# Two of sixteen states multiplied by B on GpSimd, and side work moved between product and scan

## The chip, the core and the metric

The kernel runs on one core of one Trainium2 chip. A core has five engines with queues of their own, each working in order: TensorE (PE, with its weight loads shown as PEld), VectorE (DVE), ScalarE (ACT), GpSimd (POOL) and SyncE (SP), which here issues the DMAs. They meet through semaphores. SBUF and PSUM are on-chip memories of 128 partitions; PSUM has 16 KB in each partition and all of it is in use here. The metric is the device time of one execution in microseconds (us); lower is better.

## What is computed

Four layers work on four images of 64 x 64 pixels with 96 channels. Each layer has a mixer and a quantised feed-forward block, both with a norm before and a residual after. Layer 0 has a gated mixer of its own. Layers 1 to 3, which take most of the time, have a selective scan in four directions over the 4096 pixels with 192 inner channels and 16 states. Cut to what matters:

```python
xz = x @ in_proj_w.T
xi, z = jnp.split(xz, 2, axis=-1)
...
xc = jax.nn.silu(xc)                                   # after a 3x3 depthwise convolution
x0 = xc.reshape(Bsz, Di, L)                            # pixels row by row
x1 = jnp.transpose(xc, (0, 1, 3, 2)).reshape(Bsz, Di, L)   # column by column
xs = jnp.stack([x0, x1, x0[..., ::-1], x1[..., ::-1]], axis=1)
x_dbl = jnp.einsum('bkdl,kcd->bkcl', xs, x_proj_weight)
dts, Bs, Cs = jnp.split(x_dbl, [R, R + N], axis=2)
...
dt = jax.nn.softplus(delta + delta_bias[None, :, None])
dA = jnp.exp(dt4[..., None] * A4[None, :, :, None, :])
dBu = dt4[..., None] * u4[..., None] * Bt[:, :, None, :, :]
h = a * h + b                                          # the scan along the pixels
y = jnp.einsum('lbkdn,lbkn->lbkd', hs, C_l)
return y + u * Dskip[None, :, None]
```

After the scan the four directions are added, normalised, multiplied by silu(z) and projected back to 96 channels.

## The kernel before, in words

**Stages and jobs.** Layer 0 runs first (`gated`). Then there are 12 stages, layers 1 to 3 times four images, and each is one run of scans (`scans`, line 863). Everything else that an image needs between two scans (joining the orders, mixer output, feed-forward, norm, input projection, convolution) is written as generators that stop at each `yield`; they are gathered in a `Job` (line 711) that works one image ahead. `Job.step` adds a rate, 1.4, to a credit at every scan tile and gives each of its chains one step per whole credit. At line 1006 a stage that is close to its end runs its job to completion before it loads the next image's u.

**Items and tiles.** A stage has 24 items: two directions along the pixels (`d`) x four segments of T = 1024 pixels x three chunks of channels. A chunk fills the 128 partitions with two halves of 64 channels, each with an order, 0 for rows of pixels and 1 for columns: `CHUNKS` (line 37). Chunk 1 has its halves the other way round than the other two, order 1 below. An item has 16 tiles, one for each state n, so there are 12 x 24 x 16 = 4608 scan tiles of 128 x 1024.

**A tile.** The decay `da` is an exponential on ScalarE (`decays`, line 894), two tiles ahead, into one of three SBUF buffers. B comes as a row per state; TensorE spreads it over the partitions with a selection matrix `sel` into PSUM (`b_rows`, line 900, one tile ahead; `wide()` has two PSUM buffers). `scan` (line 910) multiplies it in place by `du` and runs the scan `h`, both on VectorE. The first or last column of `h` is kept for the next segment (`carry`, ScalarE). C comes as a row too: the rows are written to DRAM (`sg.cs`), and SP reads each back spread over 64 partitions, two transfers of 256 KB a tile, two tiles ahead (`c_rows`, line 884; four buffers). GpSimd multiplies h by c in place (`times_c`, line 935), and TensorE adds it into a PSUM accumulator (`accumulate`, line 955). h has four buffers.

**The order in a step.** The loop at line 994 emits, for tile k: carry(k-1); c rows and decay of k+2; B of k+1; product and scan of k; C product of k-1; now and then a store; then the side work: one step of the preparation of the next chunk, of the next segment, and of the job (`pump(chain)`, `pump(segment)`, `work()`); last the accumulation of k-2. Every engine keeps this order, which a wrapper (`InOrder`, whose line 80 is therefore the line of all instructions in the profile) writes out by hand. Side work of VectorE thus stands after the scan of its tile.

**Preparation and side work that the change touches.** `prepare_chunk` (line 814) has four large products on GpSimd for each item, issued at steps 5, 8, 11 and 13 of the item before. `prepare_segment` (line 766) projects u to B rows, delta rows and 48 rows for C: 16 for each half of the partitions in the order 0, 1, 0, so that either order of halves finds its rows. `Norm.measure` (line 235) calls `moments` (line 217): four statistics and four aggregations in one go. `convolve` (line 568) applies Silu to two tiles, writes u to DRAM and copies it, column by column, into `cols_a` and `part_c` with three copies on GpSimd. `logarithms` (line 253) does the pending logarithms of the norms on ScalarE.

Of the kernel before, what the change touches and what calls it, by code (L numbers as in the profile page):

```python
# [20 lines left out]
C = 96  # L21
# [12 lines left out]

CHUNKS = (((0, 0), (64, 1)), ((0, 1), (64, 0)), ((128, 0), (128, 1)))


NB3 = 96  # L40
NC3 = 48
XPW = NB3 + 2 * R + NC3
W_IN = 0
# [58 lines left out]
def metaformer(ctx: ExitStack, tc: tile.TileContext, x, l0_ab, l0_rest, ssm, ffn, out):  # L102
# [61 lines left out]
    make_identity(nc, ident)  # L164
    stacked = const("stacked", [128, 64])
    dve.tensor_copy(stacked[0:64], ident[0:64, 0:64])
    dve.tensor_copy(stacked[64:128], ident[64:128, 64:128])
    twice = const("twice", [128, 128])
    dve.tensor_copy(twice[:, 0:64], stacked)
    dve.tensor_copy(twice[:, 64:128], stacked)  # L170

# [3 lines left out]
    dve.tensor_tensor(mod32, mod32, ident[0:NB3, 64:96], ALU.add)  # L175
    sel = const("sel", [NB3, NS, 192], BF16)
    for n in range(NS):
        for k in range(3):
            at = NS * (k % 2) + n
# [36 lines left out]

    def moments(src, width):

        st = sb(5, "st", [128, G, 6])
        mv = sb(5, "mv", [128, G, 2])  # L220
        for g in range(G):
            dve.bn_stats(st[:, g, :], src[:, g, 0:width])
        for g in range(G):
            dve.bn_aggr(mv[:, g, :], st[:, g, :])
        return mv

    class Norm:
# [7 lines left out]
        def measure(self, src, width, e):  # L235

            mv = moments(src, width)
            yield
            act.activation(self.v, mv[:, :, 1], AF.Identity, bias=small[e])
            act.activation(self.nm, mv[:, :, 0], AF.Copy, scale=-1.0)  # L240
            pending.append(self)

        def settle(self):

            act.activation(self.r, self.r, AF.Exp, scale=-0.5)
            yield
            refine(self.r, self.v)
            pool.tensor_tensor(self.nm, self.nm, self.r, ALU.mult)


# [161 lines left out]
    def load_y(im, s, hold):  # L412
        t = slice(s * MM, (s + 1) * MM)
        yr, yc = sb(3, "pad0", [128, MM]), sb(3, "pad1", [64, MM])
        sp.dma_start(out=yc, in_=im.y[2, 0:64, t])
        sp.dma_start(out=yr[0:64], in_=im.y[0, 0:64, t])
        sp.dma_start(out=yr[64:128], in_=im.y[1, 64:128, t])
        hold["in"][s] = yr, yc
# [17 lines left out]
    def feed_forward(im, layer, s, hold, dst):  # L436
# [49 lines left out]
        yield  # L486
        x2 = sb(1, "x2", [128, G, C])
        pool.tensor_tensor(x2, x1, y, ALU.add)
# [79 lines left out]
    def convolve(im, layer, s, hold):  # L568
# [10 lines left out]
        for i, group in enumerate(groups):  # L579
            ps = bank("conv")  # L580
            for at, (lhs, rhs) in enumerate(group):
                pe.matmul(ps, lhs, rhs, start=at == 0, stop=at == len(group) - 1)
                yield
            v = sb(1, f"u{i}", [128, MM])
            act.copy(v, ps)
            release()
            yield i == 0
            raw.append(v)
        for i, v in enumerate(raw):
            act.activation(v, v, AF.Silu, bias=w[:, W_CB + i : W_CB + i + 1])  # L590
# [5 lines left out]
        sp.dma_start(out=im.u[0, 0:64, t], in_=raw[0][0:64])  # L596
        sp.dma_start(out=im.u[1, 64:128, t], in_=raw[0][64:128])
        sp.dma_start(out=im.u[2, 0:64, t], in_=raw[1][0:64])
        for p, src, dst, c0, nc_ in (
            (slice(0, 128), raw[0], cols_a, 0, HW),  # L600
            (slice(0, 64), raw[1], part_c, 0, HW // 2),
            (slice(64, 128), raw[1], part_c, HW // 2, HW // 2),
        ):
            pool.tensor_copy(
                dst[p].rearrange("p (c r) -> p r c", r=HW)[:, SR * s : SR * s + SR, :],
                src[p].rearrange("p (r c) -> p r c", c=HW)[:, :, c0 : c0 + nc_],
            )
            if p.start or p.stop == 128:
                yield
        if s == NSTRIP - 1:  # L610
            yield
            sp.dma_start(out=im.u[1, 0:64, :], in_=cols_a[0:64])
            sp.dma_start(out=im.u[0, 64:128, :], in_=cols_a[64:128])
            for k in range(2):
                sp.dma_start(
                    out=im.u[2, 64:128, k * L // 2 : (k + 1) * L // 2],
                    in_=part_c[64 * k : 64 * k + 64],
                )

    def between(im, layer, dst=None):  # L620
# [8 lines left out]
        def first():  # L629
            if layer:  # L630
                cols_a, part_c = hold["cols"] = columns()
                sp.dma_start(out=cols_a[0:64], in_=im.y[1, 0:64, :])
# [121 lines left out]
    def load_segment(item):  # L754
# [7 lines left out]
        sg.bs = sb(2, "bs", [NB3, T], BF16)  # L762
        sg.cs = dram.tile([NC3, T], F32, tag="cs", name="cs")
        return sg

    def prepare_segment(item, sg):
# [38 lines left out]
        for k in range(2):  # L805
            cols = slice(k * MM, (k + 1) * MM)
            yield True
            ps = bank("x_proj_c")
            yield from project(ps, m, m + NC3, k)
            act.copy(sg.rows[0:NC3, cols], ps[0:NC3])  # L810
            release()
        sp.dma_start(out=sg.cs, in_=sg.rows[0:NC3])

# [49 lines left out]
    def scans(stages, jobs):  # L863
# [14 lines left out]
        drain(Chain(prepare_chunk(items[0]), True))  # L878
        tiles = [(i, n) for i in items for n in range(NS)]
        live = {}  # L880
        carries = {}
        per = 2 * NSEG * 3

        def c_rows(k):
            i, n = tiles[k]
            c = live[k, "c"] = sb(4, "c", [128, T])
            for half in range(2):
                row = NS * (CHUNKS[i.chunk][0][1] + half) + n
                sp.dma_start(
                    out=c[64 * half : 64 * half + 64],  # L890
                    in_=i.sg.cs[row : row + 1, :].to_broadcast([64, T]),
                )

        def decays(k):
            i, n = tiles[k]
            da = live[k, "da"] = sb(3, "da", [128, T])
            at = (3 * i.d + i.chunk) * NS + n
            act.activation(da, i.delta, AF.Exp, scale=weights[i.layer].decay[:, at : at + 1])

        def b_rows(k):  # L900
            i, n = tiles[k]
            b = live[k, "b"] = wide()
            swap = CHUNKS[i.chunk][0][1]
            for half in range(2):
                cols = slice(half * MM, (half + 1) * MM)
                pe.matmul(
                    b[:, cols], sel[:, n, 64 * swap : 64 * swap + 128], i.sg.bs[:, cols], start=True, stop=True
                )

        def scan(k):  # L910
            i, n = tiles[k]
# [4 lines left out]
            i.carry = carries[i.chunk]  # L916
            dve.tensor_tensor(b, i.du, b, ALU.mult)
            h = live[k, "h"] = sb(4, "h", [128, T])
# [58 lines left out]

        last = len(tiles) - 1
        chain = segment = None
        c_rows(0)  # L980
        c_rows(1)
# [12 lines left out]
        for k in range(last + 4):  # L994
            q, n = divmod(k, NS)
            if k <= last:
# [9 lines left out]
                if item.chunk == 1 and n == 4 and at(q + 2) is not None:  # L1006
# [5 lines left out]
                    segment = Chain(next_segment(items[q + 2 : q + 5]))  # L1012
                if n == 11:
                    logarithms()
                if n == 8 and nxt is not None and nxt.d == 1:
                    nxt.yf = sb(2, "y", [128, T])
                    sp.dma_start(out=nxt.yf, in_=nxt.im.y[nxt.chunk, :, nxt.seg * T : (nxt.seg + 1) * T])
            if 0 <= k - 1 <= last:
                carry(k - 1)
            if k + 2 <= last:  # L1020
                c_rows(k + 2)
                decays(k + 2)
            if k + 1 <= last:
                b_rows(k + 1)
            if k <= last:
                scan(k)
# [12 lines left out]
            if 0 <= k - 2 <= last:  # L1039
                accumulate(k - 2)  # L1040
# [278 lines left out]
def _scan(in_w, conv_w, conv_b, xp_w, dt_w, dt_b, A_logs, Ds, ln_w, ln_b, out_w):  # L1319
# [5 lines left out]
    for d in range(2):  # L1325
        for chunk, halves in enumerate(CHUNKS):
            for k, (ch, order) in enumerate(halves):
# [4 lines left out]
                v[:, NB3 + R * order : NB3 + R * order + R] = t[:, :R]  # L1332
                for s in range(3):
                    if s % 2 == order:
                        v[:, m + NS * s : m + NS * s + NS] = t[:, R + NS :]
    w[:, W_XP:W_SSM] = xp.reshape(128, -1)
# [68 lines left out]
```

## Time and profile before

| | |
|---|---|
| three runs | 20,565.64, 20,566.9 and 20,584.47 us; median 20,566.9 |
| profiled execution | 20,577.35 us; span 20,575.5 us |
| mean granted TensorE clock | 0.824 |
| first scan tile to last | 2317 to 20,104 us of the span |
| one stage of 384 tiles | 1432 to 1563 us |
| busy share of the span | DVE 87%, PE 81%, POOL 75%, ACT 60%, PEld 24% |
| C rows | 9216 transfers of 256 KB, 4.1 us from issue to landing (median) |
| bytes moved by DMA | 3149 MB |

A share of busy time is a mean over layer 0, the scans and the end. In the scan part most of VectorE's time is two large groups, product and scan; the profile gives for every group the busy time, the mean duration of one instruction in ns, and the idle time of the engine just before it with what ended most of it. In the names, buffer numbers are left out: `bc` is the PSUM tile with B, `da` the decay, `h` the scan's result, `c` the spread C row, `cs` the C rows in DRAM.

### The profile page before, as it was taken

To read this page: it belongs to the slowest core of one execution; us is meant where nothing else is said; L and a number is where in the kernel's file an instruction comes from. 1 tells how busy PE (TensorE), PEld (TensorE's weight loads), DVE (VectorE), ACT (ScalarE), POOL (GpSimd) and SP (SyncE) were. 2 spreads that over 40 slices of the span, in tenths; PEclk is the share of its full clock that TensorE was granted. 3 is DMA by queue.
4 is the path that set the end of the run, shared out by engine and by line. 5 is a ranking of instruction groups with operands and counts; after the bars stand their busy time and mean duration, and the time that the engine had idled before them with its cause. 6 is when DMAs were issued, how large, how long until landed. Compare 5 with 4: busy or idle time off the path is not lost. (4 is left out here: it accounts for less than half of the span.)

```text
span 20575.5 us, 221152 instructions
## 1 busy us (share of the span) xinstructions
PE 16595.2 (81%) x70656; PEld 4890.0 (24%) x70656; DVE 17820.2 (87%) x13851; ACT 12306.0 (60%) x19377; POOL 15531.4 (75%) x10471
## 2 busy tenths in 40 slices
PE   7888788788788887888888888887788788887876
PEld 3333212121121222222222222222222222222223
DVE  5554699999999999999999999998999999999881
ACT  3443466665665665666665665665665666666553
POOL 2332588888888887888888888887888888888882
PEclk9999888787797888787788787787897887888775
DMA  0000366667667667666667666666666666676661
GB/s 18 13 16 15 97 171 185 164 174 183 163 179 184 163 173 184 160 177 185 163 174 186 162 181 182 164 178 172 162 183 179 167 189 166 171 189 163 167 172 46
DMA packets 1234531, 3148.69 MB, mean 153 GB/s; under 512 B 428048, under 2 KB 428176, under 8 KB 1227216
## 3 DMA queue, kind: packets, MB, share of 16 engines
q1 hardware_dynamic: 1233360, 3134.55, 57.7%
q8 instruction: 555, 9.09, 0.2%
q14 instruction: 616, 5.05, 0.1%
HBM read 2819.18 MB, written 314.57 MB: 152 GB/s over the span
## 5 line engine op out<-in xcount | busy, mean ns | idle before, releaser
L80 POOL TENSOR_TENSOR h<-h,c 128x1024 f32<-128x1024 f32 (+1 forms) x4992 | 11321.2, 2274 | 4296.3 <-ACT carry L80 1700.9
L80 DVE TENSOR_TENSOR_SCAN h<-da,carry,bc 128x1024 f32<-128x1024 f32 x4608 | 10814.7, 2347 | 608.6 <-POOL carry L80 10.4
L80 PE MATMUL acc<-h,stacked 64*64 64x512 f32 x36864 | 6206.0, 750 | 499.0 <-POOL h L80 494.0
L80 ACT ACTIVATE da<-delta,decay 128x1024 f32<-128x1024 f32 x4608 | 5280.8, 1147 | 1651.2 <-DVE h L80 1603.5
L80 DVE TENSOR_TENSOR bc<-du,bc 128x1024 f32<-128x1024 f32 x4608 | 5574.9, 1210 | 607.0 <-PE bc L80 580.7
L80 PE MATMUL bc<-bs,sel 96*128 96x512 bf16 x9216 | 3359.8, 453 | 2072.3 <-DVE h L80 2055.4
L80 ACT COPY carry<-h 128x1 f32<-128x1 f32 x3456 | 648.6, 188 | 3545.9 <-DVE h L80 3541.6
L80 PEld LDWEIGHTS <-sel 96*128 96x128 bf16 x9216 | 551.5, 101 | 7014.0 <-DVE h L80 5083.4
L80 PEld LDWEIGHTS acc<-h,stacked 64*64 64x64 f32 x36864 | 1134.2, 153 | 3292.2 <-issue 1687.8
L80 ACT ACT_TABLE_LOAD x1137 | 1458.8, 1283 | 42.6 <-DVE mv L80 23.5
L80 PE MATMUL conv<-pad,tap_lo 128*128 128x512 f32 x1728 | 915.6, 628 | 0.0
L80 PE MATMUL dt_proj<-rows,w 12*128 12x512 f32 x1152 | 816.7, 795 | 0.0
L80 ACT ACTIVATE c<-acc,l_bias 128x512 f32<-128x512 f32 x384 | 263.6, 687 | 906.1 <-PE acc L80 905.6
L80 ACT ACTIVATE du<-e,ones 128x1024 f32<-128x1024 f32 x576 | 660.7, 1147 | 231.1 <-POOL delta L80 225.5
L80 PE MATMUL x_proj_b<-u,xp 128*108 128x512 f32 x1152 | 670.9, 698 | 98.1 <-DMA xp<-in_ssm 58.4
L80 PE MATMUL acc<-h,fold 128*96 128x512 f32 x768 | 416.9, 625 | 366.0 <-ACT c L80 294.4
L80 POOL TENSOR_TENSOR delta<-delta,du 128x1024 f32<-128x1024 f32 x288 | 679.3, 2359 | 12.0 <-ACT du L80 12.0
L80 POOL TENSOR_TENSOR e<-e,du 128x1024 f32<-128x1024 f32 x288 | 679.7, 2360 | 2.4 <-ACT du L80 2.4
L80 POOL TENSOR_TENSOR du<-delta,u 128x1024 f32<-128x1024 f32 x288 | 679.6, 2360 | 0.7
L80 POOL TENSOR_TENSOR delta<-delta,e 128x1024 f32<-128x1024 f32 x288 | 678.8, 2357 | 0.1
L80 PE MATMUL x_proj_c<-u,xp 128*48 128x512 f32 x1152 | 620.5, 651 | 63.4 <-ACT rows L80 63.3
L80 PE MATMUL conv<-pad,tap_hi 128*128 128x512 f32 (+1 forms) x1152 | 636.7, 647 | 8.2 <-ACT u L80 8.2
(154 smaller groups left out, 15920.2 us busy)
## 6 DMA issues: line engine op xcount, KB each, us to landing
c<-cs SPq DMA_DIRECT2D x9216, 256.0 KB, 4.1
u<-u SPq DMA_DIRECT2D x288, 512.0 KB, 7.6
y<-y SPq DMA_DIRECT2D x1152, 128.0 KB, 2.4
y<-y SPq DMA_DIRECT2D x144, 512.0 KB, 5.9
xr<-x SPq DMA_DIRECT2D x224, 192.0 KB, 4.7
u<-u SPq DMA_DIRECT2D x288, 128.0 KB, 4.6
pad<-y SPq DMA_DIRECT2D x288, 128.0 KB, 4.6
z<-zl SPq DMA_DIRECT2D x96, 256.0 KB, 2.0
```

What stands on the lines that cost most here:

```text
L80: ins = f(*a, **k).ins
```

## The change

Seven edits go together:

- States 3 and 11 (`ON_POOL`) get their B row as C gets its own: two more rows for each half in `sg.cs`, read back by SP into an SBUF tile `b` (`pool_rows`, four tiles ahead, one buffer), and GpSimd multiplies it by `du` (`times_b`, two tiles ahead). Neither TensorE's spreading nor VectorE's product is issued for these tiles.
- The decay of these tiles takes the PSUM buffer that B would have had, and is issued one tile ahead.
- Chunk 1 turns its halves round, so every chunk has order 0 below. The 48 rows become 36, `sel` shrinks from 192 to 128 columns, and u and y of chunk 1 lie the other way round in DRAM.
- The side work of a step is emitted inside `scan`, between the product and the scan. The C product of k-1, the store, and the pending logarithms move ahead of or behind neighbours in the step's order.
- `Norm.measure` yields after every second statistic.
- The convolution waits with its Silu while a step with a GpSimd product two tiles ahead is on, and the three column copies go from GpSimd to ScalarE.
- The rate of the jobs goes from 1.4 to 1.6.

```diff
-CHUNKS = (((0, 0), (64, 1)), ((0, 1), (64, 0)), ((128, 0), (128, 1)))
+CHUNKS = (((0, 0), (64, 1)), ((64, 0), (0, 1)), ((128, 0), (128, 1)))
+ON_POOL = (3, 11)
...
-NC3 = 48
-XPW = NB3 + 2 * R + NC3
+NCO = NS + len(ON_POOL)
+NC2 = 2 * NCO
+XPW = NB3 + 2 * R + NC2
...
         def measure(self, src, width, e):
 
-            mv = moments(src, width)
+            st = sb(5, "st", [128, G, 6])
+            mv = sb(5, "mv", [128, G, 2])
+            for g in range(G):
+                dve.bn_stats(st[:, g, :], src[:, g, 0:width])
+                if g % 2:
+                    yield
+            for g in range(G):
+                dve.bn_aggr(mv[:, g, :], st[:, g, :])
             yield
...
+        yield lambda: all((step["n"] + 2 - n) % NS for n in ON_POOL)
         for i, v in enumerate(raw):
             act.activation(v, v, AF.Silu, bias=w[:, W_CB + i : W_CB + i + 1])
...
-            pool.tensor_copy(
+            act.copy(
                 dst[p].rearrange("p (c r) -> p r c", r=HW)[:, SR * s : SR * s + SR, :],
...
+        def from_rows(i, dst, at):
+
             for half in range(2):
-                row = NS * (CHUNKS[i.chunk][0][1] + half) + n
+                row = NCO * half + at
                 sp.dma_start(
-                    out=c[64 * half : 64 * half + 64],
+                    out=dst[64 * half : 64 * half + 64],
                     in_=i.sg.cs[row : row + 1, :].to_broadcast([64, T]),
                 )
 
+        def on_pool(k):
+            return k <= last and tiles[k][1] in ON_POOL
+
+        def pool_rows(k):
+            i, n = tiles[k]
+            b = live[k, "b"] = sb(1, "b", [128, T])
+            from_rows(i, b, NS + ON_POOL.index(n))
+
+        def times_b(k):
+            i, b = tiles[k][0], live[k, "b"]
+            pool.tensor_tensor(b, i.du, b, ALU.mult)
+
         def decays(k):
             i, n = tiles[k]
-            da = live[k, "da"] = sb(3, "da", [128, T])
+            da = live[k, "da"] = wide() if on_pool(k) else sb(3, "da", [128, T])
...
-        def scan(k):
+        def scan(k, beside):
...
-            dve.tensor_tensor(b, i.du, b, ALU.mult)
+            if not on_pool(k):
+                dve.tensor_tensor(b, i.du, b, ALU.mult)
+            beside()
             h = live[k, "h"] = sb(4, "h", [128, T])
...
-            if 0 <= k - 1 <= last:
-                carry(k - 1)
-            if k + 2 <= last:
-                c_rows(k + 2)
-                decays(k + 2)
-            if k + 1 <= last:
-                b_rows(k + 1)
-            if k <= last:
-                scan(k)
-            if 0 <= k - 1 <= last:
-                times_c(k - 1)
-            if k >= 3 and (k - 3) % NS == NS - 1:
-                store(items[(k - 3) // NS])
-            if k <= last:
+            step["n"] = n
+
+            def beside():
                 pump(chain)
                 pump(segment)
...
+            if 0 <= k - 1 <= last:
+                carry(k - 1)
+            if on_pool(k + 1):
+                decays(k + 1)
+            if k + 2 <= last:
+                c_rows(k + 2)
+                if not on_pool(k + 2):
+                    decays(k + 2)
+            if on_pool(k + 4):
+                pool_rows(k + 4)
+            if n == 11:
+                logarithms()
+            if k + 1 <= last and not on_pool(k + 1):
+                b_rows(k + 1)
+            if 0 <= k - 1 <= last:
+                times_c(k - 1)
+            if on_pool(k + 2):
+                times_b(k + 2)
+            if k >= 3 and (k - 3) % NS == NS - 1:
+                store(items[(k - 3) // NS])
+            if k <= last:
+                scan(k, beside)
             if 0 <= k - 2 <= last:
                 accumulate(k - 2)
...
-            jobs[-1].append(Job(between(im, layer - 1), 1.4))
+            jobs[-1].append(Job(between(im, layer - 1), 1.6))
```

More of the change, by code (lines that the diff above doesn't have):

```diff
@@ L164, in metaformer @@
     make_identity(nc, ident)
-    stacked = const("stacked", [128, 64])
-    dve.tensor_copy(stacked[0:64], ident[0:64, 0:64])
-    dve.tensor_copy(stacked[64:128], ident[64:128, 64:128])
     twice = const("twice", [128, 128])
-    dve.tensor_copy(twice[:, 0:64], stacked)
-    dve.tensor_copy(twice[:, 64:128], stacked)
+    for k in range(2):
+        p = slice(64 * k, 64 * k + 64)
+        dve.tensor_copy(twice[p, 0:64], ident[p, p])
+        dve.tensor_copy(twice[p, 64:128], ident[p, p])
+    stacked = twice[:, 0:64]
     mod32 = sb(4, "h", [NB3, 32])
@@ L175, in metaformer @@
     dve.tensor_tensor(mod32, mod32, ident[0:NB3, 64:96], ALU.add)
-    sel = const("sel", [NB3, NS, 192], BF16)
+    sel = const("sel", [NB3, NS, 128], BF16)
     for n in range(NS):
-        for k in range(3):
-            at = NS * (k % 2) + n
+        for k in range(2):
+            at = NS * k + n
             dve.tensor_copy(
@@ L214, in metaformer @@
         ffw.append((w1, w2, b))
[L217 to L225, printed above, removed]
     class Norm:
@@ L248, in settle @@
             pool.tensor_tensor(self.nm, self.nm, self.r, ALU.mult)
+    step = {"n": 0}
     pending = []
@@ L416, in load_y @@
         sp.dma_start(out=yr[0:64], in_=im.y[0, 0:64, t])
-        sp.dma_start(out=yr[64:128], in_=im.y[1, 64:128, t])
+        sp.dma_start(out=yr[64:128], in_=im.y[1, 0:64, t])
         hold["in"][s] = yr, yc
@@ L486, in feed_forward @@
         yield
-        x2 = sb(1, "x2", [128, G, C])
+        x2 = sb(1, "xh", [128, G, C])
         pool.tensor_tensor(x2, x1, y, ALU.add)
@@ L596, in convolve @@
         sp.dma_start(out=im.u[0, 0:64, t], in_=raw[0][0:64])
-        sp.dma_start(out=im.u[1, 64:128, t], in_=raw[0][64:128])
+        sp.dma_start(out=im.u[1, 0:64, t], in_=raw[0][64:128])
         sp.dma_start(out=im.u[2, 0:64, t], in_=raw[1][0:64])
@@ L611, in convolve @@
             yield
-            sp.dma_start(out=im.u[1, 0:64, :], in_=cols_a[0:64])
+            sp.dma_start(out=im.u[1, 64:128, :], in_=cols_a[0:64])
             sp.dma_start(out=im.u[0, 64:128, :], in_=cols_a[64:128])
@@ L631, in first @@
                 cols_a, part_c = hold["cols"] = columns()
-                sp.dma_start(out=cols_a[0:64], in_=im.y[1, 0:64, :])
+                sp.dma_start(out=cols_a[0:64], in_=im.y[1, 64:128, :])
                 sp.dma_start(out=cols_a[64:128], in_=im.y[0, 64:128, :])
@@ L762, in load_segment @@
         sg.bs = sb(2, "bs", [NB3, T], BF16)
-        sg.cs = dram.tile([NC3, T], F32, tag="cs", name="cs")
+        sg.cs = dram.tile([NC2, T], F32, tag="cs", name="cs")
         return sg
@@ L808, in prepare_segment @@
             ps = bank("x_proj_c")
-            yield from project(ps, m, m + NC3, k)
-            act.copy(sg.rows[0:NC3, cols], ps[0:NC3])
+            yield from project(ps, m, m + NC2, k)
+            act.copy(sg.rows[0:NC2, cols], ps[0:NC2])
             release()
-        sp.dma_start(out=sg.cs, in_=sg.rows[0:NC3])
+        sp.dma_start(out=sg.cs, in_=sg.rows[0:NC2])
     def prepare_chunk(item):
@@ L879, in scans @@
         tiles = [(i, n) for i in items for n in range(NS)]
+        last = len(tiles) - 1
         live = {}
@@ L886, in c_rows @@
             c = live[k, "c"] = sb(4, "c", [128, T])
+            from_rows(i, c, n)
+        def from_rows(i, dst, at):
             for half in range(2):
-                row = NS * (CHUNKS[i.chunk][0][1] + half) + n
+                row = NCO * half + at
                 sp.dma_start(
-                    out=c[64 * half : 64 * half + 64],
+                    out=dst[64 * half : 64 * half + 64],
                     in_=i.sg.cs[row : row + 1, :].to_broadcast([64, T]),
                 )
+        def on_pool(k):
[7 more added lines that the diff above has]
+            pool.tensor_tensor(b, i.du, b, ALU.mult)
         def decays(k):
             i, n = tiles[k]
-            da = live[k, "da"] = sb(3, "da", [128, T])
+            da = live[k, "da"] = wide() if on_pool(k) else sb(3, "da", [128, T])
             at = (3 * i.d + i.chunk) * NS + n
@@ L902, in b_rows @@
             b = live[k, "b"] = wide()
-            swap = CHUNKS[i.chunk][0][1]
             for half in range(2):
@@ L906, in b_rows @@
                 pe.matmul(
-                    b[:, cols], sel[:, n, 64 * swap : 64 * swap + 128], i.sg.bs[:, cols], start=True, stop=True
+                    b[:, cols], sel[:, n, :], i.sg.bs[:, cols], start=True, stop=True
                 )
-        def scan(k):
+        def scan(k, beside):
             i, n = tiles[k]
@@ L976, in store @@
                     )
-        last = len(tiles) - 1
         chain = segment = None
+        for k in range(4):
+            if on_pool(k):
+                pool_rows(k)
         c_rows(0)
@@ L1012, in scans @@
                     segment = Chain(next_segment(items[q + 2 : q + 5]))
-                if n == 11:
-                    logarithms()
                 if n == 8 and nxt is not None and nxt.d == 1:
@@ L1332, in _scan @@
                 v[:, NB3 + R * order : NB3 + R * order + R] = t[:, :R]
-                for s in range(3):
-                    if s % 2 == order:
-                        v[:, m + NS * s : m + NS * s + NS] = t[:, R + NS :]
+                a = m + NCO * order
+                v[:, a : a + NS] = t[:, R + NS :]
+                v[:, a + NS : a + NCO] = t[:, [R + n for n in ON_POOL]]
     w[:, W_XP:W_SSM] = xp.reshape(128, -1)
```

## The prediction

> **What bounds the kernel now.** I read the engine windows first, over the stretch in which the 4608 scan tiles run (2317 to 20104 us of the span); then the groups of that stretch; then VectorE's and GpSimd's timelines of quiet items; then what VectorE waits for.
>
> ```profile
> 2317.00:20104.00 17787.00, 14464.76 (x64882) 3985.83 (x64886) 16550.66 (x11837) 11256.41 (x17217) 14713.98 (x8972) 0.81 0.66 174
> ```
>
> The columns are length, then busy time of PE, PEld, DVE, ACT and POOL, the granted clock, the DMA share and GB/s. VectorE is busy for 93% of the stretch, GpSimd for 83%: one engine is the bound and a second stands close behind it. The groups say with what:
>
> ```profile
> L80 DVE TENSOR_TENSOR_SCAN h<-da,carry,bc 128x1024 f32<-128x1024 f32 x4608 | 10814.7, 2347 | 608.6 <-POOL carry L80 10.4 <-ACT da L80 8.8 <-DVE bc L80 3.3
> L80 DVE TENSOR_TENSOR bc<-du,bc 128x1024 f32<-128x1024 f32 x4608 | 5574.9, 1210 | 607.0 <-PE bc L80 580.7 <-POOL du L80 23.3 <-POOL carry L80 0.6
> ...
> L80 POOL TENSOR_TENSOR h<-h,c 128x1024 f32<-128x1024 f32 x4607 | 10833.3, 2358 | 2821.6 <-ACT carry L80 1700.9 <-DVE h L80 366.9 <-DMA c<-cs 293.6
> ```
>
> Per tile VectorE makes the product with B (1210 ns) and the scan (2347 ns); GpSimd makes the product with C (2358 ns) and is idle 2822 us before it, mostly because the scan has not ended. A quiet stretch shows the pitch:
>
> ```profile
> 5003.11 1.21 DVE L80 TENSOR_TENSOR bc<-du,bc 128x1024 f32<-128x1024 f32 x1
> 5004.45 2.35 DVE L80 TENSOR_TENSOR_SCAN h<-da,carry,bc 128x1024 f32<-128x1024 f32 x1
> 5006.71 1.21 DVE L80 TENSOR_TENSOR bc<-du,bc 128x1024 f32<-128x1024 f32 x1
> ```
>
> Start to start, product to scan takes 1.34 us (1.21 and a pause of 0.13, as the scan reads what the product writes) and scan to product 2.26: 3.605 per tile over the stretch. 4608 x 3.605 = 16,612 us. VectorE's other groups of the stretch (norm statistics, the subtraction on the B rows, the fp8 cast, a residual) sum to 586 us. Those leave 17,787 - 16,612 - 586 = 589 us, and the wait list names them:
>
> ```profile
> DVE bc L80 <- PE bc L80: 580.7, 351, 17.9
> DVE xq L80 <- PE ff_xt L80: 24.7, 30, 1.9
> ```
>
> So today VectorE hardly ever waits for a producer of side work.
>
> **The products leave VectorE.** Two tiles of 16, so 288 x 2 = 576 of 4608, lose the 1.34 us step: 576 x 1.345 = -775 us. Their scan now reads the decay from PSUM and b from SBUF, before it was the reverse. The nearest row, 2347 ns with one operand on each side, gives 0 for the swap; a bound from the shorter scan of layer 0 (1280 ns for 512 columns, 2.50 ns a column against 2.29) would be 576 x 0.21 = 121 us at most. I take 0.
>
> The row first: that scan, with one matrix operand in SBUF, runs beside GpSimd's product, and neither is longer for it (2.34 us on GpSimd at 8031.58, with VectorE idle, against a mean of 2358 ns). The Trainium skill, "SBUF — State Buffer", section "Who interferes with whom", says that a VectorE instruction with two SBUF inputs and a GpSimd one that reads SBUF block each other for a whole instruction. By that rule a decay kept in SBUF would lose about 576 x 2.35 = 1354 us, an estimate from it; with the decay in PSUM the rule gives 0, as the row does. No trace here has the two-input scan.
>
> **What GpSimd takes on.** 576 products du x b. Back to back, GpSimd's 128x1024 products start 2.315 us apart:
>
> ```profile
> 5034.45 2.36 POOL L80 TENSOR_TENSOR delta<-delta,du 128x1024 f32<-128x1024 f32 x1
> 5036.77 2.35 POOL L80 TENSOR_TENSOR h<-h,c 128x1024 f32<-128x1024 f32 x1
> ```
>
> That is +1333 us of work. The column copies of the convolution go to ScalarE: GpSimd loses 96 x (1.07 + 2 x 0.62) = 222 us, ScalarE gains 125 (at the 0.58 us of its 512-column copies) to 222 (at GpSimd's own price); ScalarE is busy 11,256 of 17,787 us, which hides them. An item of 16 tiles then asks GpSimd for 16 + 4 + 2 large products, 22 x 2.315 = 50.9 us, plus 4.1 of side work at its rows' prices; VectorE for 14 x 3.605 + 2 x 2.26 + 2.0 = 57.0. It fits, with 2.0 us to spare.
>
> But the product has a due time. It is issued two steps ahead, behind the C product of its step. Counted from the end of the scan before: hand-off 0.25, C product 2.3, B product 2.3, so ready at 4.9 us; two whole tiles later, at 7.2, it is needed. The margin is 2.3 us, and one chunk-preparation product just before (step 8, for state 11) takes 1.3 of it. Carrying GpSimd's work from step to step at row prices, in the built order, 59 of 576 are late, by 67 us together. Bounds 0 and 576 x 0.25; I take +50.
>
> Behind each such product on GpSimd stands the next C product, which releases the c buffer for SP and the h buffer; four of each cover about 8 us.
>
> **PE, ScalarE, DMA.** PE loses 1152 B matmuls (453 ns); it was busy 81%, so 0. The decay of a GpSimd tile is issued one step ahead, not two: from the end of the scan before, copy 0.19 and exponential 1.15 are done at 1.6 us, needed at 3.6; ScalarE idles before that copy 1.0 us on the mean (3545.9 over 3456), so 0; without cover it is late by what ScalarE has in hand, 1.3 us for a table load. SP issues 1152 more row transfers of 256 KB, 9% more bytes at a DMA share of 0.66: asked four steps ahead, they land in 4.1 us, so 0.
>
> **Side work between product and scan.** It gains the 0.13 pause in steps that hold VectorE side work. In the built order 577 steps held some, now 953 (the statistics are split in pairs over two steps), 844 of them with a product: 844 x 0.13 = -110 us. It costs where the producer is late, since the scan used to cover that:
>
> ```profile
> 8215.21 2.35 DVE L80 TENSOR_TENSOR_SCAN h<-da,carry,bc 128x1024 f32<-128x1024 f32 x1
> ...
> 8216.28 0.46 ACT L80 COPY yt<-y_t 128x384 f32<-128x384 f32 x1
> ...
> 8217.47 1.11 DVE L80 BATCH_NORM_STATS2 st<-yt 128x6 f32<-128x192 f32 x4
> ...
> 8218.78 1.21 DVE L80 TENSOR_TENSOR bc<-du,bc 128x1024 f32<-128x1024 f32 x1
> ```
>
> The product of this tile ended at 8215.07, the copy that the statistics read at 8216.74. Now they wait for nothing; placed before the scan, they and the scan stand 1.5 us. I did this for each kind in the trace (producer's end minus product's end, cut at the scan's 2.25 us) and counted kinds in the new order: fp8 cast after its transposes, 105 x 1.15 = 121 us; statistics on x2, whose GpSimd add is now in the same step 65 times (3 before), 65 x 2.25 = 146, else 13; on y, 60 x 0.90 + 6; out_proj residual, 37 x 1.90 + 8 (8 such before); B-row subtraction 25. Sum 445 us. Of the bounds 0 (all of it taken out of the 581 us that VectorE waits for PE anyhow) and 445 I take +350, nearer to the row-by-row count.
>
> **Job pace.** The job rate goes from 1.4 to 1.6, but the split statistics need more rounds: in the seven stages where a job has the most rounds (indices 4 to 10) the writes of the next image's columns move from step 350 to 355 of its 384, and step 356 loads u behind them on the SP queue:
>
> ```profile
> 10969.06 1.23 SPq L80 DMA_DIRECT2D u<-cols_a  x2
> 10970.82 4.45 SPq L80 DMA_DIRECT2D u<-part_c  x2
> 10975.36 10.97 SPq L80 DMA_DIRECT2D c<-cs  x8
> ```
>
> The writes land 13 us later. Today VectorE does not feel it there; where job and load already met (stages 3 and 7) one tile waited 18 us. One stage of the seven (10) has its wait of 17.6 already. So 6 x (0 to 18); I take 6 x 10 = +60, as no new weights are loaded there.
>
> **Sum.** The profiled execution took 20,577 us (span 20,575.5). -775 + 50 - 110 + 350 + 60 = -425: 20,152. Its time is 10 above the median of the three runs and inside their range; less 10, 20,140.
>
> **Rivals.**
> *The side work waits for nothing that counts.* For it: VectorE's 581 us of PE waits can absorb such stalls. Against: the ends in the trace. -775 - 110 + 50 + 60 - 10 gives 19,790.
> *Two engines tie.* GpSimd's sum, 14,714 + 1333 - 222 plus a hand-off of 0.25 us at 4608 tiles (1152), is 16,977; VectorE's, 16,612 - 775 + 586 + 589, is 17,012. When neither has slack, GpSimd's 294 us of waits for C rows, now hidden, add to the forecast: 20,430. Against: the queue of four h and c buffers.
> *Slower: the scan hostage to side work.* Each of the 953 steps stands before its scan. I counted 0.47 us each and took 0.37; it turns slower at (775 + 110 - 50 - 60) / 953 = 0.81. At 1.1 us, if a fuller GpSimd and ScalarE deliver later than in this trace, it costs 1048: 20,840. For it: GpSimd's queue is longer in just those steps. Against: most producers of the B-row subtraction end 2.3 us before the product does.
> *The change does not do what it says* would need the 576 products still on VectorE; the built order has 4032 there, so it gets no chance.
>
> **How the numbers follow.** Forecast 0.54, own range 19,950 to 20,330; no side stalls 0.20; tie 0.15; slower 0.11. The range from 19,730 (the first rival, less its boundary term) to 20,550 (the tie plus the swap's bound of 121) leaves out the slower case and some of each tail. A measurement tells 0.2% (41 us) from no change: faster 0.85, same 0.04, slower 0.11.
>
> **What would show it.** In the new profile: 4032 products and 4608 scans on VectorE, scan still at 2347 ns; 576 GpSimd products at 2.36 us; scan-to-scan of 2.26 us where the next tile is GpSimd's; VectorE idle before xq, st and x summing to about 350 us (rivals: under 100, over 900); VectorE waits for GpSimd's b near 50; waits for PE bc still near 580; a pause near step 360 in stages 4 to 9. A scan longer with its decay in PSUM, or GpSimd products over 2.4 us, would break the first term.

## The result, and the profile after

The changed kernel takes 21,375 us (median of four runs, 21,362 to 21,378) against 20,576 for the kernel before on the same chip: 1.039 times as long, 95% interval 1.037 to 1.041. I had forecast 20,140. The change also puts x2 into the buffer of xh, which the list of edits does not name. First the window of the scan tiles after the change, columns as before (length; busy PE, PEld, DVE, ACT, POOL; clock; DMA share; GB/s):

```profile
2388.00:20863.00 18475.00, 14392.65 (x63583) 3942.72 (x63583) 15802.91 (x11233) 11413.30 (x17465) 15835.05 (x9263) 0.79 0.72 183
```

VectorE is busy 748 us less, near the 775 of the product term, and GpSimd 1121 us more (1111 expected). But the stretch is 688 us longer, so VectorE stands idle 1436 us more than before. Neither engine is full any longer: both are busy for 86% of it. VectorE's groups of instructions in the changed kernel (busy time, mean ns of one | idle time ahead of them and what ended most of it):

```profile
L80 DVE TENSOR_TENSOR_SCAN h<-da,carry,bc 128x1024 f32<-128x1024 f32 x4032 | 9444.5, 2342 | 573.4 <-POOL carry L80 167.3 <-ACT da L80 11.6 <-DVE bc L80 5.2
L80 DVE TENSOR_TENSOR bc<-du,bc 128x1024 f32<-128x1024 f32 x4031 | 4875.8, 1210 | 1105.5 <-PE bc L80 1102.3 <-POOL h L80 1.6
L80 DVE TENSOR_TENSOR_SCAN h<-bc,carry,b 128x1024 f32<-128x1024 f32 x576 | 1342.5, 2331 | 117.6 <-POOL b L80 83.6 <-ACT bc L80 21.0 <-PE acc L80 5.0
...
L80 DVE BATCH_NORM_STATS2 st<-xh 128x6 f32<-128x96 f32 x352 | 72.9, 249 | 490.1 <-POOL xh L80 490.1
L80 DVE CAST xq<-ff_xt 96x512 fp8e5<-96x512 f32 x105 | 71.8, 684 | 174.9 <-PE ff_xt L80 174.8
...
L80 DVE TENSOR_TENSOR x<-xr,out_proj 128x384 f32<-128x384 f32 x81 | 44.4, 548 | 145.4 <-PE out_proj L80 141.3 <-DMA c<-cs 4.2
```

The instructions cost what was said: 576 scans read the decay from PSUM in 2331 ns (2342 for the others), 4032 products stay. What grew is the idle time ahead of them: for B from TensorE 581 to 1102 us, for the statistics on x2 3 to 490, for the cast 25 to 175, for the residual 7 to 141, and 10 to 167 for the clearing of a carry. Two of these waits before the change (who waits, for whom; sum in us, count, longest; scan part):

```profile
DVE x L80 <- PE out_proj L80: 7.3, 5, 2.2
DVE st L80 <- POOL x L80: 3.0, 3, 1.1
```

GpSimd's new product takes 2398 ns, 40 more than its C product, and its wait for its rows is small (GpSimd's groups of the changed kernel, with shapes kept apart; columns as before):

```profile
L80 POOL TENSOR_TENSOR h<-h,c 128x1024 f32<-128x1024 f32 x4608 | 10816.0, 2358 | 2474.5 <-ACT carry L80 1459.0 <-DMA c<-cs 366.3 <-issue 186.6
...
L80 POOL TENSOR_TENSOR b<-du,b 128x1024 f32<-128x1024 f32 x576 | 1381.1, 2398 | 28.2 <-DMA b<-cs 26.9 <-POOL h L80 0.2
```

GpSimd is idle 2475 us before its C products, more than half of it until ScalarE's copy of the carry, which itself waits for the scan to end: two engines near full that wait for each other. The worst kind of wait shows how (timeline of the change):

```profile
7128.42 1.21 DVE L80 TENSOR_TENSOR bc<-du,bc 128x1024 f32<-128x1024 f32 x1
...
7130.56 1.34 POOL L80 TENSOR_TENSOR ff_y<-ff_y,b 128x96 f16<-128x96 f16 x4
...
7131.86 2.37 POOL L80 TENSOR_TENSOR h<-h,c 128x1024 f32<-128x1024 f32 x1
...
7134.19 2.41 POOL L80 TENSOR_TENSOR b<-du,b 128x1024 f32<-128x1024 f32 x1
...
7136.55 0.91 POOL L80 TENSOR_TENSOR xh<-x,ff_y 128x384 f32<-128x384 f32 x1
...
7137.49 0.42 DVE L80 BATCH_NORM_STATS2 st<-xh 128x6 f32<-128x96 f32 x2 [7.87 <-POOL xh L80]
7137.83 2.33 DVE L80 TENSOR_TENSOR_SCAN h<-da,carry,bc 128x1024 f32<-128x1024 f32 x1
```

The product of the tile ends at 7129.6. The scan could follow, but the statistics on x2 are in between; x2 is added on GpSimd behind a C product and a B product. VectorE stands 7.87 us, and no scan ends meanwhile that would give GpSimd its next C product.

Below, "excess" at tile n is the distance from the last scan's start to this one's, less the undisturbed 3.605 us (2.26 without a product), summed over all items by the scans' starts in the trace. It is 1176 us before and 2639 after.

### The profile page after: what moved, and what is told of

Read it like the earlier page. It is cut to its first block, busy times and chain, and to the rows that moved or that the text cites. A ratio compares the mean times of both kernels' runs of the same rounds, so it can differ in the third digit from the quotient of the medians.

```text
span 21373.6 us, 221522 instructions
## 1 busy us (share of the span) xinstructions
PE 16591.8 (78%) x69504; PEld 4883.2 (23%) x69504; DVE 17077.9 (80%) x13259; ACT 12484.6 (58%) x19674; POOL 16646.7 (78%) x10759
## 5 line engine op out<-in xcount | busy, mean ns | idle before, releaser
L80 DVE TENSOR_TENSOR_SCAN h<-da,carry,bc 128x1024 f32<-128x1024 f32 x4032 | 9444.5, 2342 | 573.4 <-POOL carry L80 167.3
L80 PE MATMUL acc<-h,twice 64*64 64x512 f32 x36864 | 6320.5, 763 | 909.0 <-POOL h L80 905.0
L80 DVE TENSOR_TENSOR bc<-du,bc 128x1024 f32<-128x1024 f32 x4032 | 4877.0, 1210 | 1128.8 <-PE bc L80 1102.3
L80 ACT ACTIVATE da<-delta,decay 128x1024 f32<-128x1024 f32 x4032 | 4607.5, 1145 | 959.0 <-DVE h L80 937.6
L80 PE MATMUL bc<-bs,sel 96*128 96x512 bf16 x8064 | 3017.3, 463 | 1875.7 <-DVE h L80 1860.5
L80 PEld LDWEIGHTS acc<-h,twice 64*64 64x64 f32 x36864 | 1157.9, 156 | 3833.7 <-POOL h L80 2010.5
L80 PEld LDWEIGHTS <-sel 96*128 96x128 bf16 x8064 | 489.0, 102 | 6247.9 <-DVE h L80 3810.0
L80 DVE TENSOR_TENSOR_SCAN h<-bc,carry,b 128x1024 f32<-128x1024 f32 x576 | 1342.5, 2331 | 117.6 <-POOL b L80 83.6
L80 POOL TENSOR_TENSOR b<-du,b 128x1024 f32<-128x1024 f32 x576 | 1381.1, 2398 | 28.2 <-DMA b<-cs 26.9
L80 ACT ACTIVATE bc<-delta,decay 128x1024 f32<-128x1024 f32 x576 | 641.7, 1114 | 428.2 <-DVE h L80 427.8
```

The lines of the kernel that those rows point to most:

```text
L80: ins = f(*a, **k).ins
```

## The experiments

Theory 1: the place of the side work makes the engines wait for each other. Theory 2: GpSimd is too full, and its lag is paid by all. Each diff is against the changed kernel or the run named.

**Undo the two main parts, alone and together.** `a_no_pool`:

```diff
-ON_POOL = (3, 11)
+ON_POOL = ()
```

> No state on GpSimd (all 16 products on VectorE again); everything else of the change stays, the side work between product and scan among it. Theory 1 (the place of the side work makes VectorE and GpSimd wait for each other; waits for xh, xq, x, the carry memset and much of PE bc come from it): the saving of 775 us is lost and most of the waits stay, 21,500 to 22,000 us, with VectorE's waits for POOL xh, xq, x and carry together still above 700 us. Theory 2 (GpSimd is too full with 576 more products, and its lag makes all others late): the waits go, 20,500 to 20,750 us.

`b_side_after`:

```diff
-            beside()
             h = live[k, "h"] = sb(4, "h", [128, T])
...
                 op1=ALU.add,
             )
+            beside()
```

> Only the place of the side work is undone: it is emitted after the scan again; the 576 products stay on GpSimd. Theory 1: 19,950 to 20,350 us, faster than both kernels, VectorE's waits for POOL xh, xq and x together under 200 us. Theory 2: 21,000 to 21,400 us, with PE bc waits still near 1,100 us.

`c_both_undone` has both edits.

> No state on GpSimd and the side work after the scan. What is left of the change: the halves of chunk 1, statistics in pairs, rate 1.6, copies on ScalarE, x2 in the buffer of xh, the C product and the carry memset in their new order. Both theories: within 1% of before, 20,450 to 20,750 us. If it is slower than 20,900, the cause is in these small edits and neither theory holds.

`d_side_pace` adds to b:

```diff
             for g in range(G):
                 dve.bn_stats(st[:, g, :], src[:, g, 0:width])
-                if g % 2:
-                    yield
...
-            jobs[-1].append(Job(between(im, layer - 1), 1.6))
+            jobs[-1].append(Job(between(im, layer - 1), 1.4))
```

> As the run with the side work after the scan, and also the statistics in one go and the rate 1.4 again. If the statistics and the rate are of no account, within 60 us of that run; if the late writes of u columns at the stage ends cost what I booked for them, 40 to 100 us less.

Measured: a 21,159 us (1.028 times before, interval 1.027 to 1.030), b 21,076 (1.024, 1.022 to 1.025), c 20,925 (1.017, 1.015 to 1.018), d 20,715 (1.006, 1.005 to 1.008). No theory had this. The place of the side work costs 235 us without and 300 with products on GpSimd, so theory 1 is true but small; the products save nothing even with the side work after the scan (b against c: +151); and the statistics and the rate, which I had thought small, cost 361 us (b against d). VectorE's waits in d from 2390 to 20,100 us (who waits, for whom; sum in us, count, longest) show that those for side work are gone and those for B are not:

```profile
DVE bc L80 <- PE bc L80: 1091.4, 545, 27.0
DVE h L80 <- POOL b L80: 148.6, 91, 7.8
DVE h L80 <- POOL carry L80: 140.7, 64, 6.2
DVE st L80 <- POOL xh L80: 56.7, 27, 3.8
DVE xq L80 <- PE ff_xt L80: 32.2, 30, 2.1
```

**Statistics or rate.** `n_rate_16` is b with the statistics in one go, at rate 1.6.

> The change with the side work after the scan and the statistics in one go, at rate 1.6. It splits the 360 us between the run at 21,076 (pairs, 1.6) and that at 20,715 (one go, 1.4). If the pairs cost, through statistics that come in one step with their producer: 20,700 to 20,800. If the denser job costs: 20,950 to 21,100.

20,824 us (1.012, 1.011 to 1.014): the pairs cost 252, the rate 109. I counted 65 steps in the changed kernel's order (3 before) in which the first two statistics of x2 stand with the add on GpSimd that they read. These waits grow with the rate first (d, n, b, whole execution):

```profile
DVE st L80 <- POOL xh L80: 62.6, 31, 3.8
```

```profile
DVE st L80 <- POOL xh L80: 183.8, 71, 6.7
```

```profile
DVE st L80 <- POOL xh L80: 258.9, 82, 5.4
```

The pairs are therefore mostly something else. In the profiled executions b is 223 us longer than n: 40 of it lie ahead of the first scan tile (2327 to 2367 us of the span), 86 behind the last, and 97 between. Of the stage ends (tiles 340 to 383) alone, the excess is 64 us more in b. Why the beginning and the end grew was not tested. Nor was TensorE's granted clock the same: its mean over the execution is 0.80 to 0.81 in a, b, c and n (0.800 after the change), all at rate 1.6, and 0.820 in d and 0.824 before, and TensorE's passes for B take 464 ns in n against 451 in d. No run separates that from the rate.

**Where the products' gain goes.** From here on all runs but q and t have d's three edits. `e_acc_later`:

```diff
-        for k in range(last + 4):
+        for k in range(last + 5):
...
-            if k >= 3 and (k - 3) % NS == NS - 1:
-                store(items[(k - 3) // NS])
+            if k >= 4 and (k - 4) % NS == NS - 1:
+                store(items[(k - 4) // NS])
...
-            if 0 <= k - 2 <= last:
-                accumulate(k - 2)
+            if 0 <= k - 3 <= last:
+                accumulate(k - 3)
```

> The run with side work after the scan, statistics in one go and rate 1.4 (20,715 us), with one edit: the accumulation of a tile is issued one step later (k-3 in place of k-2), and the store with it. Theory 3 (a late C product on GpSimd holds TensorE's queue at the accumulation, and the B of a later tile stands behind it): VectorE's waits for PE bc fall from 1,091 us to under 700, TensorE's waits for POOL h from 1,101 to under 500, time 20,150 to 20,450. Theory 2 (GpSimd is simply full; whoever waits for it only moves): the waits come back as waits for h buffers or b, 20,600 to 20,800.

`f_memset`, where `clear` is the carry's tile and memset taken out of `scan`:

```diff
+            if k <= last:
+                clear(k)
             if 0 <= k - 1 <= last:
                 times_c(k - 1)
```

> The same 20,715 us run with the clearing of a new carry issued ahead of the C product on GpSimd's queue, where it was before the change. The scan's waits for POOL carry, 141 us in 64 waits, go to under 20; time 20,560 to 20,640 if nothing else was late at those tiles, no change if the next wait takes their place.

`g_no_pool_pace` is d with `ON_POOL = ()`.

> The same 20,715 us run with no state on GpSimd: the price of the products alone, without the side work's place, the split statistics and the rate. What stays of the change is the halves of chunk 1, the copies on ScalarE, x2 in the buffer of xh, and the order of the carry's clearing. Theory 3 and theory 2 both: PE bc waits near 580 us; time 20,650 to 20,800 (before plus 130 for the carry), so that the 775 us taken from VectorE were lost whole to GpSimd's lag. If it is 21,000 or more, the products do save time and the small edits cost more than I think.

`h_acc_memset` has the edits of e and f.

> Both edits on the 20,715 us run: accumulation one step later, and the carry cleared ahead of the C product. Theory 3: the two add up, 20,000 to 20,350 us, faster than both kernels. Theory 2: 20,500 to 20,700.

Measured: e 21,299 us (1.035, 1.034 to 1.037), f 20,617 (1.002, 1.001 to 1.003), g 20,782 (1.010, 1.008 to 1.011), h 21,244 (1.032, 1.031 to 1.034). The carry's clearing is worth 98 us, as expected. Against g the 576 products bring 67 us, not 775. And e, made to give B its way, is 584 us slower. Its longest wait of VectorE has changed its name (the view of VectorE's waits of run e, from 2390 to 20,100 us; the columns are the sum in us, the count and the longest):

```profile
DVE h L80 <- PE acc L80: 1681.8, 781, 26.1
```

B is waited for 10 us in the whole execution; the scan waits for its h buffer, which is free only when TensorE has accumulated the tile four back. Four h buffers do not bear a step more of lag. Theory 3 in that form falls; that the fault is GpSimd's lag or TensorE's queue stays.

**Without GpSimd's product, and one state.** `j_no_product`, on f:

```diff
         def times_b(k):
-            i, b = tiles[k][0], live[k, "b"]
-            pool.tensor_tensor(b, i.du, b, ALU.mult)
+            pass
```

> The 20,617 us run (side work after the scan, old pace, carry cleared early), with the 576 products du x b on GpSimd left out: the scans of states 3 and 11 read the spread B rows as they come, so that part of the result is not computed. All transfers, orders and PSUM buffers stay. Theory 2 (the 1,381 us of products fill GpSimd, and its lag is paid by all others): 19,800 to 20,000 us, PE bc waits under 700, TensorE's waits for POOL h under 500. If the loss comes from something else of the new order (the decay in PSUM, the missing product as cover for TensorE, more DMA), 20,400 or more.

`k_state_11` is f with `ON_POOL = (11,)`.

> The 20,617 us run with one state on GpSimd, 11, in place of two. If the loss grows with GpSimd's load alone, half the products give half of what two give, 20,600 to 20,650 us (two states gave 65 us less 100 of the carry against none). If it is state 3 that hurts, as the excess at tile 4 (436 us, against 36 at tile 12) says, 20,300 to 20,450 us, faster than before.

j 20,294 us (0.986, 0.985 to 0.988), between the two expectations: GpSimd's work costs 324 us, and as much again is lost without it. k 20,659 (1.004, 1.003 to 1.005): one state brings as little as two, so that state 3 alone is not the culprit that I took it for.

The excess by tile says that the two states lose in different places. State 11 loses at its own tile, where the scan waits for GpSimd's late product: 242 us in f and 219 in k, but 94 in j, which leaves that product out, and 74 in the run m below, with all products on VectorE. VectorE's wait for it in f, from 2390 to 20,100 us:

```profile
DVE h L80 <- POOL b L80: 162.8, 107, 7.8
```

State 3 loses at the tile behind it: the excess at tile 4 is 436 us in f and still 417 in j, against 181 in m and 169 in k. GpSimd's B product cannot be blamed there, and between the scans of tiles 2 and 4 TensorE waits for GpSimd's h in none of the 288 items of j. A quiet item of j, around tile 4 (its timeline: start, length, engine, instruction, and the wait ahead of it in brackets):

```profile
4925.20 1.91 PE L80 MATMUL x_proj_c<-u,xp 128*36 128x512 f32 x4
...
4926.08 2.32 DVE L80 TENSOR_TENSOR_SCAN h<-bc,carry,b 128x1024 f32<-128x1024 f32 x1
...
4927.03 1.09 PE L80 MATMUL acc<-y,twice 64*64 64x512 f32 x8
...
4927.94 1.04 PE L80 MATMUL acc<-h,twice 64*64 64x512 f32 x8
...
4928.91 0.60 PE L80 MATMUL bc<-bs,sel 96*128 96x512 bf16 x2
...
4929.56 1.23 DVE L80 TENSOR_TENSOR bc<-du,bc 128x1024 f32<-128x1024 f32 x1 [1.15 <-PE bc L80]
```

The scan is tile 3's. It came 1.34 us sooner, for want of a product, but TensorE has the same list to do before tile 4's B: a projection and the start of an accumulator, 16 passes. VectorE gives back 1.15 of 1.34 us.

Not every item is like this one. TensorE can start an accumulator only when ScalarE has copied the last one out (y), and with state 3 on GpSimd ScalarE has two decays ahead of that copy, those of tiles 3 and 4, in place of one. TensorE's waits for that copy, j first, then m:

```profile
PE acc L80 <- ACT y L80: 397.3, 192, 6.6
```

```profile
PE acc L80 <- ACT y L80: 85.6, 84, 4.3
```

They are 92 us in k, without state 3. In j the 192 items with such a wait lose 1.41 us each at tile 4 and the other 96 lose 1.53 us, so that ScalarE's list and TensorE's are both in it, and no run parts them. Theory 2 had also expected TensorE's waits for GpSimd's h to fall under 500 us in j: they are 759 (1150 in f, 376 in m), so GpSimd's C products still come late at other tiles.

**The place of the two states.** `o_states_2_7` is f with `ON_POOL = (2, 7)`; `p_2_7_no_barrier` drops the yield ahead of the Silu from it; `q_after_2_7` is the whole change with these states. (With state 2 the step counter that the Silu looks at starts at 3, as at 0 it would hold it for ever.)

```diff
-        yield lambda: all((step["n"] + 2 - n) % NS for n in ON_POOL)
```

> The 20,617 us run (side work after the scan, old pace, carry cleared early) with states 2 and 7 on GpSimd in place of 3 and 11. Their products are issued at steps 0 and 5, ahead of or far behind the preparation products (5, 8, 11, 13), and tile 4 follows a tile with a product of its own, so that TensorE has a whole tile's time after the step in which it starts an accumulator (step 2). Theory 4 (what was lost is the place: TensorE's accumulator start behind state 3, GpSimd's preparation before state 11): excess at tile 4 falls from 436 us to about 200 and VectorE's waits for b from 163 to under 50; 20,100 to 20,400 us, faster than before. If the loss is in any tile without a product, the excess comes back at tiles 3 and 8: 20,550 to 20,700.

> The same with states 2 and 7, and without the extra yield that holds the convolution's Silu. The yield costs a job step for each strip even when it does not hold, and puts the last u writes of stages 4 to 9 at the loads of u. If that is what these stages lose at tile 361 (5 to 9 us each), 50 to 120 us less than the run with the yield; if the Silu's burst on ScalarE hurts more, it is slower.

> The change as it is, with states 2 and 7 in place of 3 and 11 and nothing else altered: how much of the change's loss is in the choice of the two states. Theory 4 with the gain found above carried over: 20,950 to 21,150 us against 21,375; if side work in between and pairs rule, within 100 us of 21,375.

o 20,940 us (1.018, 1.016 to 1.019), p 20,885 (1.015, 1.014 to 1.017), q 21,729 (1.056, 1.055 to 1.057). Theory 4 falls: the excess at tile 4 stays (452 us), and tiles 7 (365, against 50) and 9 (636, against 267) join it. Without the yield (p) the run is 55 us shorter. A new wait is in part for the decay of a tile without a product, issued one step ahead in place of two (waits of VectorE in run o, from 2390 to 20,100 us, columns as above):

```profile
DVE h L80 <- ACT bc L80: 173.6, 41, 9.1
```

My cover for that, ScalarE idle 1.0 us on the mean, did not hold there.

**What is left.** `m_rest_undone`: no states on GpSimd, f's clearing, copies on GpSimd, x2 in a buffer of its own.

> No state on GpSimd, side work after the scan, old pace, carry cleared early, the column copies on GpSimd again and x2 in a buffer of its own. What stays is the turned halves of chunk 1 and the C product emitted before the scan. 20,540 to 20,620 us, as before: then the 205 us of the run without products came from the carry, the copies and the shared buffer. If 20,700 or more, the halves or the order cost.

`r_rest_no_barrier` drops the same yield from m.

> The run with the rest undone (20,736 us) without the extra yield in the convolution. What stays of the change is the turned halves and the C product emitted ahead of the scan, which changes no engine's own order. 20,560 to 20,630 us, as before; 20,680 or more would say that the halves or something not yet named cost 100 us.

m 20,736 us (1.008, 1.006 to 1.009), r 20,585 (1.000, 0.999 to 1.001). The turned halves and the C product's new place cost nothing; the yield, which never holds in m, costs 151 us as one more step for each strip. At the stage ends (tiles 340 to 383) 62 of it show, the rest lies elsewhere in the stages.

**TensorE relieved.** `s_half_acc` on f, and `t_before_half_acc` on the kernel before:

```diff
-        def add_quarters(i, v, lhs, start, stop):
+        def add_quarters(i, v, lhs, start, stop, n=0):
 
-            for k in range(2):
+            for k in range(2 if n in (0, NS - 1) else 1):
...
-            add_quarters(i, h, stacked, False, n == NS - 1)
+            add_quarters(i, h, stacked, False, n == NS - 1, n)
```

> The 20,617 us run (states 3 and 11 on GpSimd, side work after the scan, old pace, carry cleared early) with TensorE relieved: states 1 to 14 add only the first half of their pixels into the accumulator, two of four passes, so part of the result is not computed. All waits and orders stay. Theory 5 (TensorE's queue, 81% busy and in order, is the second bound: in steps with side work it fills the time that VectorE gives up): 19,950 to 20,200 us, PE bc waits under 600. If it falls no more than its control, the rest is GpSimd's lag and not TensorE's own work.

> Control: the kernel before with the same relief (states 1 to 14 add only the first half of their pixels, part of the result is not computed). VectorE is the bound there and waits 581 us for B; theory 5 gives 20,300 to 20,480 us. A fall as large as in the other run would say that TensorE's load costs both alike and does not explain why the products bring so little.

s 20,610 us (1.002, 1.001 to 1.003), t 20,567 (1.000, 0.999 to 1.001): nothing moved. But nothing was relieved either. The accumulation's group, f first and then s:

```profile
L80 PE MATMUL acc<-h,twice 64*64 64x512 f32 x36864 | 6159.0, 745 | 1156.3 <-POOL h L80 1149.8
```

```profile
L80 PE MATMUL acc<-h,twice 64*64 64x512 f32 x20736 | 6143.1, 758 | 1131.3 <-POOL h L80 1125.1
```

16,128 passes fewer, and 16 us less busy. So these runs do not test theory 5, which stays open.

## Why the prediction was wrong, by its own steps

The runs make a chain from before to after, one part at a time (medians, us). They are from several chips, on which the kernel before took 20,569 to 20,591 us, so a step of less than some 20 us cannot be told from none:

| step | run | change | I had taken |
|---|---|---|---|
| rest: halves, order of the C product | r 20,585 | 0 | 0 |
| extra yield in the convolution | m 20,736 | +151 | 0 |
| copies to ScalarE, shared buffer, carry cleared late | g 20,782 | +46, of it the carry +98 | 0 |
| 576 products to GpSimd | d 20,715 | -67 | -725 |
| rate 1.6 | n 20,824 | +109 | +60, with the pairs |
| statistics in pairs | b 21,076 | +252 | (in the 60) |
| side work between product and scan | after 21,375 | +300 | +240 |

The sizes depend on the order of the chain. In the changed kernel the products cost 216 us (after against a) and with the side work after the scan 151 (b against c); the pairs and the rate together cost 143 us without products (c against g) and 361 with them.

**The products** is the step that failed most: by 658 us in this chain, by 941 in the changed kernel. The 1.345 us each is right where nothing else is going on: over tiles 304 to 352 of the first three stages, with the job done, an item takes 55.7 to 56.3 us in the change against 58.3 to 58.9 before, 2.6 us for two products. It is wrong in steps with side work. I wrote "PE loses 1152 B matmuls (453 ns); it was busy 81%, so 0": a mean where the margin of a step decides. TensorE works in order, and the B of the next tile stands behind what side work and accumulation put there; with a product gone VectorE arrives 1.34 us sooner at a queue that is no shorter. The waits for PE bc are 990 us in j, 725 in m. The decay one step ahead, which I also put at 0, may have a part in that: TensorE's waits for the copy of y behind it are 397 us in j, 86 in m. The second half is "I take +50" for GpSimd's late products, measured as 324 (f against j). The wait for b alone is 163 us in f (84 in the changed kernel). The rest I had not priced: TensorE's accumulation waits for the C product, with the next B behind it, and TensorE waits for GpSimd's h 1150 us in f and 759 in j (905 after the change, 494 before).

**The job pace**: I priced the late writes of u at the stage ends (+60, for six stages, though stage 7 already had its wait). There I had the mechanism and nearly the size: tile 361 of stages 4, 5, 6, 8 and 9 has 41 us of excess after the change, 7 to 10 us each, and none before. What I left at nothing is all else that the pace does: 151 us for the yield, 109 for the rate and 252 for the pairs, of which the stage ends are a part. With the rate the statistics of x2 wait 184 us for their producer in place of 63 (n and d); I had counted that wait in the side work's sum and nowhere else, although it comes with the side work after the scan too.

**The carry**: the C product was moved ahead of `scan`, and with it ahead of the memset inside it on GpSimd's queue. My sum had no term for this: 2.4 us at 71 items, 167 us of wait in the change, 98 us by f.

**The side work** held: +240 taken, +300 measured (235 without products), and most of the kinds that I named wait. The 350 was a choice between 0 and 445 (its terms add up to 443), so a part of the closeness is luck: the waits are 5.6 us for x2 and not 2.25, with a longer queue on GpSimd (3.5 us in a, without the B product), while those for y are 10 us and not 60.

**The swap of decay and b between SBUF and PSUM** cost nothing, as its row said: 2331 ns for these scans, 2347 before, with GpSimd's C product at 2358 in both. That agrees with the rule that I cited; no run has the decay in SBUF, so what the rule says of that case is not tested.

**The rivals**: the slower one had the right sign and, with its side waits, a part of the cause, but at 0.11 and with the wrong main term. "Two engines tie" was nearest in mechanism: I had seen that both sums come to 17,000 us and priced only 294 us of it.

**Open**: how the 333 us that are lost without GpSimd's product (775 less 442 against m) divide between TensorE's list and ScalarE's. 236 of them are excess at tile 4, but no run has taken either list away. (m also has the column copies on GpSimd and x2 in a buffer of its own; by the chain these two are worth about -50 us, so the loss may be nearer 385.) No version run here that has states on GpSimd beats the kernel before and could stand for it: f comes nearest (1.002), and j leaves out part of the computation. f without the yield was not run; by o against p (55 us) and m against r (151) it would take 20,466 to 20,562 us, an estimate, a little less than the kernel before.

## What to carry to other kernels

Time taken from the busiest engine was worth here what the next queue's margin allowed in that step, not what its mean idle share suggested: for every shortened tile, list what must still be issued in order before the next one, on each engine. With a second engine at the first one's load (both at 86% here), a wait of either became a wait of both, so work that both need belongs where its producer is long done. And a yield or a statement moved in a hand-written order is a change of its own: one yield that never held cost 0.7%, one memset behind a product 0.5%.

## What the runs showed that I had not expected

TensorE's 64x64 passes on different quadrants run side by side: in f four of them start within 0.04 us of each other (at 5020.11), and with 16,128 of 36,864 left out the group is busy 6143 us in place of 6159, so here the count of passes says nothing of their cost. And run j, in which GpSimd's product was left out and all transfers were kept, shows that 9% more bytes by DMA (share 0.66 before, 0.75 in j in the scan part) cost little: VectorE waited for the b rows 12 us in it, and GpSimd for C rows 379 us (298 in m).
